# A state-space scan kernel: sums over states by four transposes each, and the token convolution of four chunks on PE

## The chip, the cores and the metric

The kernel runs on one core of one Trainium2 chip. The metric is the device time of one launch in microseconds (us), the median of several runs; a separate execution of the same program is profiled. The engines are PE (TensorE, matmuls; PEld is its loading of weights), DVE (VectorE), ACT (ScalarE), POOL (GpSimd) and SP (SyncE, which issues most DMAs).

## The reference

Four images of 384 channels and 48 x 48 positions pass through four layers, each after a group normalisation and with a residual: a selective state-space block, a block with a patch-wise spectral filter and a 3 x 3 depthwise convolution, an 11 x 11 depthwise convolution, and a mixture of four experts. The change touches the first layer alone (L is 2304 positions, 768 inner channels, 16 states):

```python
xz = xs @ in_proj_w.T
xin, z = jnp.split(xz, 2, axis=-1)
xc = ... # causal convolution over tokens, 4 taps, one filter a channel
xin = jax.nn.silu((xc + conv_b[None, :, None]).transpose(0, 2, 1))
x_dbl = xin @ x_proj_w.T
dt, Bm, Cm = jnp.split(x_dbl, [DT_RANK, DT_RANK + D_STATE], axis=-1)
dt = jax.nn.softplus(dt @ dt_proj_w.T + dt_proj_b)
A = -jnp.exp(A_log)
def step(h_prev, inp):
    x_t, dt_t, B_t, C_t = inp
    dA = jnp.exp(dt_t[..., None] * A)
    dBx = dt_t[..., None] * B_t[:, None, :] * x_t[..., None]
    h_new = dA * h_prev + dBx
    y_t = jnp.einsum('bds,bs->bd', h_new, C_t)
    return (h_new, y_t)
...
y = ys.transpose(1, 0, 2) + xin * D
y = y * jax.nn.silu(z)
out = y @ out_proj_w.T        # then a layer norm over channels
```

All arithmetic is in float32.

## The kernel before

The 2304 positions of an image are cut into five chunks (four of 460, one of 464), and the 768 inner channels into six tiles of 128, taken in three pairs. A list G holds the 20 (image, chunk) items. For each item the generator `scans` runs 96 state steps (`unit`): 3 pairs x 16 states x 2 tiles of the pair. One step is: ACT makes da = exp(dt A) into one of two PSUM banks (L626); POOL multiplies u by the broadcast row B (L630); DVE runs the recurrence (L634) into da or into g; the product with C goes into one of six g buffers, on DVE (L640) for two steps of three and on POOL (L651) for the third; ACT saves the last column for the next chunk (L642, L650). PE then adds g to y: `summed` multiplies it by the identity matrix and accumulates in the PSUM bank of that tile, tag y0 or y1, one buffer each (L600). The skip term xin D is one more matmul of that sum, with a diagonal matrix `d_diag` as weights. Sums of steps that POOL multiplied are held back in `late`. When a pair is done, `gate` (L659) multiplies y in place by the silu of z, on DVE, out of the same bank; the bank is free for the next pair then.

Around the steps, `plan` hangs pieces of other work on step numbers: the tail of the chunk before (`gate` of its last pair, `out_proj`, `layer_norm`, `residual`), `project` and `project_z` for the next chunk and this one, `gates` (the silus, L535 and L538), `expand` and `steps`. In `project`, three matmuls (L490) make the rows of a tile with three tokens of halo in a bank, ACT takes the last tap with the bias (L502), and DVE adds the other three taps (L507, three instructions). `bank` hands out two PSUM banks for all of this. Two more banks serve the other three layers of the image before (`later`, L782) and the experts of the one before that (`experts`, L1090): their pieces are spread over the 480 steps of an image by hand-set weights. So the first image has steps alone, the second has layers two and three beside them, and the third and fourth the experts too. After the last step only layers of the last two images remain.

The code order gives the priority; the framework's scheduler may take a piece that is ready earlier or later than it stands, and each engine then works through its own list in order. `after` fixes the order of two instructions on one engine.

Of the kernel before, what the change touches and what calls it, by code (L numbers as in the profile page):

```python
# [16 lines left out]
P = 128  # L17
# [8 lines left out]
TT = 4  # L26
# [18 lines left out]
def tile_layers(ctx: ExitStack, tc: tile.TileContext, a: dict, out: bass.AP):  # L45
# [218 lines left out]
    with ExitStack() as first:  # L264
# [29 lines left out]
        d_diag = wp.tile([P, MT, P], F32, name="d_diag")  # L294
        for m in range(MT):
            nc.scalar.activation(d_diag[:, m, :], ident, AF.Copy, scale=d_col[:, m : m + 1])
# [117 lines left out]
        def scans(wk, mm):  # L414
# [5 lines left out]
            G = [(b, t) for b in range(NB) for t in range(NC)]  # L420
            st = [{} for _ in G]
# [58 lines left out]
            def project(i, j):  # L480
# [20 lines left out]
                acc = c["xc"][:, j, :n]  # L501
                nc.scalar.activation(  # L502
# [87 lines left out]
            def summed(i, m, lhsT, src):  # L590

                (b, t), c = G[i], st[i]
                n = CHUNKS[t]
                if ("y", m) not in c:
                    c["y", m] = mm.tile(
                        [P, 512], F32, name=f"y{b}_{t}_{m}", tag=f"y{m % 2}", bufs=1
                    )
                    c["terms", m] = 0
                c["terms", m] += 1
                return nc.tensor.matmul(  # L600
                    c["y", m][:, :n],
                    lhsT=lhsT,
                    rhs=src,
                    start=c["terms", m] == 1,
                    stop=c["terms", m] == DS + 1,
                    skip_group_check=True,
                )

            def skip(i, p):

                (b, t), c = G[i], st[i]
                for m in (2 * p, 2 * p + 1):
                    summed(i, m, d_diag[:, m, :], c["xc"][:, m, : CHUNKS[t]])

            def unit(i, m, s):
# [23 lines left out]
                if here is da:  # L639
# [3 lines left out]
                    ins = summed(i, m, ident, g[:, :n])  # L643

                    c["since"] = c.get("since", 0) + 1
                    if late and (c["since"] >= 2 or (m % 2 and s == DS - 1)):
                        after(late.pop(0)(), ins)
                else:
# [3 lines left out]
                    late.append(lambda: summed(i, m, ident, g[:, :n]))  # L652
                    c["since"] = 0

            def gate(i, m):
                (b, t), c = G[i], st[i]
                n = CHUNKS[t]
                zm = c["zs"][:, m, :n]
                nc.vector.tensor_tensor(zm, c["y", m][:, :n], zm, ALU.mult)  # L659
# [56 lines left out]
            def tail(i):  # L716

                for k in range(TT):
                    yield lambda k=k: out_proj(i, k)
                yield lambda: layer_norm(i)  # L720
                for ct in range(CT):
                    yield lambda ct=ct: residual(i, ct)
# [3 lines left out]
            load(0)  # L726
            for j in range(MT):
                project(0, j)
            gates(0, None)
            expand(0)  # L730
            steps(0, 0)
            for i, (b, t) in enumerate(G):
                todo = {}
# [11 lines left out]
                if i:  # L745
                    for m in (MT - 2, MT - 1):
                        plan(0, lambda m=m: gate(i - 1, m))
                    for k, piece in enumerate(tail(i - 1)):
                        plan(3 + 2 * k, piece)
# [13 lines left out]
                for p in range(MT // 2):  # L763
                    if p:
                        for h in range(2):
                            plan(2 * DS * p, lambda m=2 * p - 2 + h: gate(i, m))
                    if p < MT // 2 - 1:
                        plan(2 * DS * p + DS, lambda p=p: steps(i, p + 1))
                    plan(2 * DS * p + DS, lambda p=p: skip(i, p))
                for p in range(MT // 2):  # L770
                    for q in range(2 * DS):
# [3 lines left out]
                        yield b, t, 2 * DS * p + q  # L775
                assert not todo
            for m in (MT - 2, MT - 1):
                gate(len(G) - 1, m)
# [575 lines left out]
```

## Time and profile before

Columns of the shares: busy time of an engine as a share of the span.

| what | value |
|---|---|
| runs | 5764.69, 5762.97, 5753.89 us; median 5762.97 |
| profiled execution | 5767.51 us, span 5765.7 us, 69035 instructions |
| PE, PEld | 5255.3 us (91%), 3320.9 us (58%), 23236 instructions each |
| DVE | 4030.3 us (70%) |
| ACT | 2956.1 us (51%) |
| POOL | 3110.3 us (54%) |
| granted clock of PE, mean | 0.953 |
| sums over states, L600 | 3840 instructions of PE for g, 240 for the skip term |
| state steps, L626 | 1920 exponentials |
| first scan, last exponential start | at 96 us, at 4860 us |

The page adds up busy time over stages of different character; from about 1030 us on, other layers run beside the scan, and from 4870 us on there is no scan. A line such as L600 collects all instructions of one code line, with the shape of their operands, how often they ran, their busy time and mean duration, and the idle time of their engine just before them.

### The profile page before, as it was taken

How to read it: one execution, taken by the hardware profiler on the slowest of the kernel's cores; microseconds unless marked ns; L12 is line 12 of the kernel's file. 1: busy time of each engine (PE TensorE's matmuls, PEld its weight loads, DVE VectorE, ACT ScalarE, POOL GpSimd, SP SyncE). 2: the span in 40 equal slices, each digit the busy share in tenths (PEclk: the TensorE clock that was granted, in tenths of full speed). 3: DMA queues.
4: the chain of work that ended last, by engine and by line, in shares of the span. 5: the costliest groups of instructions: out<-in, count | busy, mean ns of one | idle time of the engine just before them, and what ended most of it. 6: DMA issues, size and time to landing. Idle time of an engine off the chain costs nothing. (4 is left out here: it accounts for less than half of the span.)

```text
span 5765.7 us, 69035 instructions
## 1 busy us (share of the span) xinstructions
PE 5255.3 (91%) x23236; PEld 3320.9 (58%) x23236; DVE 4030.3 (70%) x5653; ACT 2956.1 (51%) x6424; POOL 3110.3 (54%) x2795
## 2 busy tenths in 40 slices
PE   6888888988889999999887999999988799999999
PEld 3333333433455546777433664877634375789999
DVE  5988988899997796666899577656698856451110
ACT  3555555555566654444655565444455564335321
POOL 3877888766586685555565366545465646000000
PEclk9999989988999999999998899999989899899999
DMA  4444444434344363233333235323332323311100
GB/s 135 134 137 135 143 127 139 124 118 121 118 139 137 114 206 108 89 106 112 112 119 106 90 120 171 99 88 102 103 112 95 121 93 125 114 45 43 54 23 26
DMA packets 396011, 634.19 MB, mean 110 GB/s; under 512 B 32373, under 2 KB 386789, under 8 KB 392190
## 3 DMA queue, kind: packets, MB, share of 16 engines
q1 hardware_dynamic: 382148, 618.58, 33.7%
q10 hardware_dynamic: 13498, 11.11, 0.7%
q8 instruction: 184, 3.01, 0.2%
q14 instruction: 181, 1.48, 0.1%
HBM read 571.80 MB, written 57.80 MB: 109 GB/s over the span
## 5 line engine op out<-in xcount | busy, mean ns | idle before, releaser
L630 POOL TENSOR_TENSOR bu<-u,bc 128x460 f32<-128x460 f32 (+1 forms) x1920 | 2217.2, 1167 | 1346.3 <-DVE g L634 632.8
L600 PE MATMUL y<-g,ident 128*128 128x460 f32 (+1 forms) x3840 | 1838.3, 597 | 286.8 <-DVE g L640 282.2
L626 ACT ACTIVATE da<-dt,a_neg 128x460 f32<-128x460 f32 (+1 forms) x1920 | 1232.1, 646 | 268.5 <-DVE g L640 166.2
L634 DVE TENSOR_TENSOR_SCAN da<-da,carry,bu 128x460 f32<-128x460 f32 (+1 forms) x1008 | 1165.7, 1170 | 196.6 <-ACT da L626 170.1
L600 PEld LDWEIGHTS y<-g,ident 128*128 128x128 f32 x3840 | 704.3, 201 | 1008.1 <-DVE g L640 541.7
L651 POOL TENSOR_TENSOR g<-g,bc 128x460 f32<-128x460 f32 (+1 forms) x660 | 766.7, 1162 | 249.4 <-DVE g L634 128.0
L640 DVE TENSOR_TENSOR g<-da,bc 128x460 f32<-128x460 f32 (+1 forms) x1260 | 775.9, 627 | 109.7 <-PE y L600 80.1
L634 DVE TENSOR_TENSOR_SCAN g<-da,carry,bu 128x460 f32<-128x460 f32 (+1 forms) x528 | 617.2, 1169 | 134.1 <-PE y L600 67.9
L1139 PEld LDWEIGHTS ph<-xe,w 128*128 128x128 f32 x4608 | 596.7, 191 | 54.3 <-issue 40.4
L1157 PEld LDWEIGHTS pout<-hr,w 128*128 128x128 f32 x4608 | 591.4, 190 | 54.7 <-issue 43.8
L1139 PE MATMUL ph<-xe,w 128*128 128x144 f32 x4608 | 620.1, 288 | 0.0
L1157 PE MATMUL pout<-hr,w 128*128 128x144 f32 x4608 | 616.4, 287 | 1.5 <-DVE xe L1168 1.5
L642 ACT COPY carry<-da 128x1 f32<-128x1 f32 x1008 | 158.0, 157 | 884.2 <-DVE g L640 882.5
L998 PEld LDWEIGHTS pc<-band,row 128*128 128x128 f32 x3456 | 455.8, 194 | 81.1 <-issue 48.6
L1147 ACT ACTIVATE hr<-ph,nb 128x144 f32<-128x144 f32 x768 | 235.5, 377 | 507.3 <-PE ph L1139 506.9
L998 PE MATMUL pc<-band,row 128*128 128x162 f32 (+14 forms) x3456 | 469.2, 286 | 6.5 <-ACT row L987 4.7
L669 PE MATMUL po<-w_out,zs 128*115 128x384 f32 (+1 forms) x960 | 346.6, 494 | 11.1 <-DVE zs L659 7.7
L878 DVE SCALAR_TENSOR_TENSOR dw<-pad,w_dw,dw 128x384 f32<-128x384 f32 x576 | 342.2, 609 | 14.4 <-ACT pad L866 11.2
L634 DVE TENSOR_TENSOR_SCAN da<-da,nil,bu 128x460 f32<-128x460 f32 x252 | 291.5, 1170 | 74.3 <-ACT da L626 66.4
L490 PE MATMUL pin<-xch,w_inx 128*128 128x463 f32 (+2 forms) x720 | 323.1, 579 | 10.8 <-DVE dt L585 4.7
L518 PE MATMUL pinz<-xch,w_inz 128*128 128x460 f32 (+1 forms) x720 | 306.0, 559 | 12.0 <-DVE xc L507 7.9
L507 DVE SCALAR_TENSOR_TENSOR xc<-pin,conv_w,xc 128x460 f32<-128x460 f32 (+1 forms) x360 | 246.9, 686 | 76.6 <-ACT xc L502 73.9
(170 smaller groups left out, 4754.8 us busy)
## 6 DMA issues: line engine op xcount, KB each, us to landing
bc<-bcd SPq DMA_DIRECT2D x768, 460.0 KB, 3.6
bc<-bcd SPq DMA_DIRECT2D x192, 464.0 KB, 3.6
xs<-x1d SPq DMA_DIRECT2D x24, 576.0 KB, 4.3
x2d<-xs SPq DMA_DIRECT2D x24, 576.0 KB, 2.9
x<-x2d SPq DMA_DIRECT2D x12, 1152.0 KB, 6.5
x3d<-x SPq DMA_DIRECT2D x12, 1152.0 KB, 5.9
xg<-x3d SPq DMA_DIRECT2D x24, 576.0 KB, 4.6
xe<-x3d SPq DMA_DIRECT2D x64, 216.0 KB, 2.6
```

The costliest lines, as they stand in the source:

```text
L490: nc.tensor.matmul(ps[:, lo : halo + n], lhsT=w_inx[:, k, bass.ts(j, P)], rhs=c["x"][:, k, lo : halo + n], start=k == 0, stop=k == CT - 1,)
L600: return nc.tensor.matmul(c["y", m][:, :n], lhsT=lhsT, rhs=src, start=c["terms", m] == 1, stop=c["terms", m] == DS + 1, skip_group_check=True,
L626: nc.scalar.activation(da[:, :n], c["dt", p][:, m % 2, :n], AF.Exp, scale=a_neg[:, m, s : s + 1])
L630: nc.gpsimd.tensor_mul(bu[:, :n], c["u", p][:, m % 2, :n], bc[:, 0, :n])
L634: nc.vector.tensor_tensor_scan(here[:, :n], da[:, :n], bu[:, :n], last if t else nil[:, 0:1], ALU.mult, ALU.add,)
L640: nc.vector.tensor_mul(g[:, :n], here[:, :n], bc[:, 1, :n])
L651: nc.gpsimd.tensor_mul(g[:, :n], here[:, :n], bc[:, 1, :n])
L669: nc.tensor.matmul(ps[:w, :C], lhsT=c["zs"][:, m, bass.ts(k, w)], rhs=w_out0[:, m, :], start=m == 0, stop=m == MT - 1,)
L878: nc.vector.scalar_tensor_tensor(v, src, w_dw[:, ct, k : k + 1], v, ALU.mult, ALU.add)
L998: nc.tensor.matmul(d["acc2"][:, : BANDS[k] * W].rearrange("p (h w) -> p h w", w=W)[:, lo - edges[k] : hi - edges[k], xlo:xhi], lhsT=d["row ...
L1139: nc.tensor.matmul(ps[:, bass.ts(m, EB)], lhsT=d["w1"][:, e, k, bass.ts(m, P)], rhs=d["x", s][:, k, :], start=k == 0, stop=k == CT - 1,)
L1157: nc.tensor.matmul(d["o"][:, bass.ts(m, EB)], lhsT=d["w2"][:, e, k, bass.ts(m, P)], rhs=d["h", s, e][:, k, :], start=e == 0 and m == 0 and ...
```

## The change

The diagonal `d_diag` goes. A new helper `turned` sends a tile to PE as four transposes: each takes a quarter of the columns (115 or 116) as weights, the identity as the moving operand, and adds into the y bank, which now holds tokens on partitions and four blocks of 128 channels. `skip` scales xin by D on ACT into a g buffer and starts the sum with it; it now stands ahead of the pair's steps. The sum of every state step uses `turned`. After the pair's last step `collect` moves the two y banks to SBUF on ACT, and `gate`, a few steps later, transposes them back into one of the two shared banks and multiplies there. In chunks 1 to 4 of the first image, `project` has ACT copy the rows with their halo to SBUF, PE apply the four taps with diagonal matrices (24 of them, made once by ACT), and ACT add the bias.

```diff
-        d_diag = wp.tile([P, MT, P], F32, name="d_diag")
-        for m in range(MT):
-            nc.scalar.activation(d_diag[:, m, :], ident, AF.Copy, scale=d_col[:, m : m + 1])
...
                 acc = c["xc"][:, j, :n]
+                if "diag" in taps and t:
+                    row = taps["pool"].tile([P, halo + TM], F32, name=f"row{b}_{t}_{j}", tag="row")
+                    nc.scalar.copy(row[:, : halo + n], ps[:, : halo + n])
+                    qs = bank(f"pcv{b}_{t}_{j}")
+                    for k in range(DCONV):
+                        nc.tensor.matmul(
+                            qs[:, :n],
+                            lhsT=taps["diag"][:, j, k, :],
+                            rhs=row[:, k : k + n],
+                            start=k == 0,
+                            stop=k == halo,
+                        )
+                    nc.scalar.activation(
+                        acc, qs[:, :n], AF.Identity, bias=d["cb"][:, j : j + 1]
+                    )
+                    return
...
-            def summed(i, m, lhsT, src):
+            def turned(y, src, n, start, stop):
+
+                w = n // TT
+                return [
+                    nc.tensor.matmul(
+                        y[:w, bass.ts(k, P)],
+                        lhsT=src[:, bass.ts(k, w)],
+                        rhs=ident,
+                        is_transpose=True,
+                        start=start and k == 0,
+                        stop=stop,
+                        skip_group_check=True,
+                    )
+                    for k in range(TT)
+                ]
+
+            def skip(i, p):
...
+                for h in range(2):
+                    m = 2 * p + h
+                    y = c["y", m] = mm.tile(
+                        [P, 512], F32, name=f"y{b}_{t}_{m}", tag=f"y{h}", bufs=1
+                    )
+                    dx = wk.tile([P, TM], F32, name=f"dx{b}_{t}_{m}", tag="g", bufs=6)
+                    nc.scalar.activation(
+                        dx[:, :n], c["xc"][:, m, :n], AF.Copy, scale=d_col[:, m : m + 1]
+                    )
+                    turned(y, dx, n, True, False)
...
-                    ins = summed(i, m, ident, g[:, :n])
-
-                    c["since"] = c.get("since", 0) + 1
-                    if late and (c["since"] >= 2 or (m % 2 and s == DS - 1)):
-                        after(late.pop(0)(), ins)
+                    ins = turned(c["y", m], g, n, False, s == DS - 1)
+
+                    c["since"] += 1
+                    if late and (c["since"] == 2 or (m % 2 and s == DS - 1)):
+                        for one in late.pop()():
+                            after(one, ins[-1])
                 else:
...
-                    late.append(lambda: summed(i, m, ident, g[:, :n]))
+                    late.append(lambda: turned(c["y", m], g, n, False, s == DS - 1))
                     c["since"] = 0
+
+            def collect(i, p):
+                (b, t), c = G[i], st[i]
+                w = CHUNKS[t] // TT
+                for h in range(2):
+                    m = 2 * p + h
+                    yt = c["yt", m] = wk.tile([P, 512], F32, name=f"yt{b}_{t}_{m}", tag="yt")
+                    nc.scalar.copy(yt[:w, :], c["y", m][:w, :])
 
             def gate(i, m):
...
+                ps = bank(f"pyb{b}_{t}_{m}")
+                for k in range(TT):
+                    nc.tensor.transpose(
+                        ps[:, bass.ts(k, w)], c["yt", m][:w, bass.ts(k, P)], ident[:w, :w]
+                    )
                 zm = c["zs"][:, m, :n]
-                nc.vector.tensor_tensor(zm, c["y", m][:, :n], zm, ALU.mult)
+                nc.vector.tensor_tensor(zm, ps[:, :n], zm, ALU.mult)
...
+            taps["diag"] = taps["pool"].tile([P, MT, DCONV, P], F32, name="diag", bufs=1)
+            for j in range(MT):
+                for k in range(DCONV):
+                    nc.scalar.activation(
+                        taps["diag"][:, j, k, :], ident, AF.Copy, scale=conv_w[:, j, k : k + 1]
+                    )
             for i, (b, t) in enumerate(G):
+                if b == 1 and t == 0:
+                    taps.clear()
+                    first_image.close()
...
                 if i:
-                    for m in (MT - 2, MT - 1):
-                        plan(0, lambda m=m: gate(i - 1, m))
                     for k, piece in enumerate(tail(i - 1)):
-                        plan(3 + 2 * k, piece)
+                        plan(2 + 2 * k, piece)
...
-                            plan(2 * DS * p, lambda m=2 * p - 2 + h: gate(i, m))
+                            plan(2 * DS * p + 3 + 3 * h, lambda m=2 * p - 2 + h: gate(i, m))
                     if p < MT // 2 - 1:
                         plan(2 * DS * p + DS, lambda p=p: steps(i, p + 1))
-                    plan(2 * DS * p + DS, lambda p=p: skip(i, p))
                 for p in range(MT // 2):
+                    skip(i, p)
                     for q in range(2 * DS):
                         unit(i, 2 * p + q % 2, q // 2)
                         for piece in todo.pop(2 * DS * p + q, []):
                             piece()
                         yield b, t, 2 * DS * p + q
+                    collect(i, p)
```

`tail` now begins with the two gates of the last pair, two steps apart.

More of the change, by code (lines that the diff above doesn't have):

```diff
@@ L420, in scans @@
             G = [(b, t) for b in range(NB) for t in range(NC)]
+            first_image = ExitStack()
             st = [{} for _ in G]
@@ L588, in steps @@
                     nc.gpsimd.tensor_mul(u[:, h, :n], dt[:, h, :n], c["xc"][:, 2 * p + h, :n])
-            def summed(i, m, lhsT, src):
+            def turned(y, src, n, start, stop):
[13 more added lines that the diff above has]
+            def skip(i, p):
                 (b, t), c = G[i], st[i]
                 n = CHUNKS[t]
-                if ("y", m) not in c:
-                    c["y", m] = mm.tile(
-                        [P, 512], F32, name=f"y{b}_{t}_{m}", tag=f"y{m % 2}", bufs=1
-                    )
[L598 to L613, printed above, removed]
+                for h in range(2):
+                    m = 2 * p + h
+                    y = c["y", m] = mm.tile(
+                        [P, 512], F32, name=f"y{b}_{t}_{m}", tag=f"y{h}", bufs=1
+                    )
+                    dx = wk.tile([P, TM], F32, name=f"dx{b}_{t}_{m}", tag="g", bufs=6)
[3 more added lines that the diff above has]
+                    turned(y, dx, n, True, False)
             def unit(i, m, s):
@@ L657, in gate @@
                 n = CHUNKS[t]
+                w = n // TT
+                ps = bank(f"pyb{b}_{t}_{m}")
[3 more added lines that the diff above has]
+                    )
                 zm = c["zs"][:, m, :n]
-                nc.vector.tensor_tensor(zm, c["y", m][:, :n], zm, ALU.mult)
+                nc.vector.tensor_tensor(zm, ps[:, :n], zm, ALU.mult)
             def out_proj(i, k):
@@ L716, in tail @@
             def tail(i):
+                yield lambda: gate(i, MT - 2)
+                yield lambda: gate(i, MT - 1)
                 for k in range(TT):
@@ L726, in scans @@
             load(0)
+            taps = {"pool": first_image.enter_context(tc.tile_pool(name="taps", bufs=2))}
             for j in range(MT):
@@ L775, in scans @@
                         yield b, t, 2 * DS * p + q
+                    collect(i, p)
                 assert not todo
-            for m in (MT - 2, MT - 1):
-                gate(len(G) - 1, m)
             for piece in tail(len(G) - 1):
```

## The prediction

> **What bounds the kernel now.** I read the busy table by stretches first, because the page's averages (PE 91%, DVE 70%) mix stages. I cut the span where the character of the work changes.
>
> ```profile
> core 0: us, PE busy (x) PEld busy (x) DVE busy (x) ACT busy (x) POOL busy (x), PEclk, DMA share, GB/s
> 110.00:1030.00 920.00, 758.77 (x1793) 325.71 (x1794) 817.85 (x1019) 497.76 (x1051) 760.24 (x677) 0.94 0.43 135
> 1030.00:1700.00 670.00, 591.59 (x1736) 283.92 (x1735) 615.74 (x877) 394.89 (x845) 455.22 (x410) 0.93 0.40 123
> 1700.00:2200.00 500.00, 478.57 (x1877) 271.65 (x1876) 418.17 (x551) 312.93 (x643) 366.86 (x327) 0.98 0.46 149
> 2200.00:2750.00 550.00, 547.69 (x3069) 417.13 (x3068) 341.11 (x447) 252.73 (x630) 293.25 (x263) 0.99 0.33 101
> 2750.00:3250.00 500.00, 418.66 (x1198) 202.10 (x1197) 425.94 (x623) 278.08 (x572) 289.58 (x261) 0.88 0.36 112
> 3250.00:3600.00 350.00, 341.65 (x1567) 213.28 (x1567) 246.61 (x336) 210.65 (x410) 199.91 (x177) 0.99 0.41 134
> 3600.00:4150.00 550.00, 547.78 (x3072) 418.87 (x3071) 335.50 (x438) 252.71 (x630) 294.14 (x263) 0.99 0.31 97
> 4150.00:4600.00 450.00, 372.23 (x936) 165.75 (x935) 399.66 (x579) 245.44 (x498) 269.68 (x243) 0.89 0.34 110
> 4600.00:4850.00 250.00, 241.93 (x1362) 177.36 (x1361) 170.48 (x211) 170.16 (x339) 149.90 (x132) 0.99 0.33 108
> ```
>
> Columns: stretch, length, busy time and count of each engine, granted clock, DMA. There are three kinds. In 2200 to 2750 and 3600 to 4150 (experts beside the scan) PE is busy all but 2 us of 550: PE time is kernel time. In 1700 to 2200, 3250 to 3600 and 4600 to 4850 PE is busy 96 to 98%, which counts latencies too; DVE's chain shares the limit. Elsewhere DVE leads: 818 of 920 us (89%) in the first image, POOL close behind with 760 (83%), PE 759 (82%).
>
> How many state steps (one exponential of L626 each) fall into the PE-led stretches, from that line's busy time alone:
>
> ```profile
> 1700.00:2200.00 500.00, 145.25 (x227) 0.98 0.46 149
> 2200.00:2750.00 550.00, 117.48 (x182) 0.99 0.33 101
> 3250.00:3600.00 350.00, 77.99 (x122) 0.99 0.41 134
> 3600.00:4150.00 550.00, 117.48 (x182) 0.99 0.31 97
> 4600.00:4870.00 270.00, 64.44 (x101) 0.99 0.34 112
> ```
>
> 364 steps where PE is full, 450 where it is nearly so, 1106 in DVE-led stretches.
>
> **What one sum costs PE.** The groups come next, for the counts:
>
> ```profile
> L600 PE MATMUL y<-g,ident 128*128 128x460 f32 (+1 forms) x3840 | 1838.3, 597 | 286.8 <-DVE g L640 282.2
> L626 ACT ACTIVATE da<-dt,a_neg 128x460 f32<-128x460 f32 (+1 forms) x1920 | 1232.1, 646 | 268.5 <-DVE g L640 166.2
> ```
>
> 1920 steps, but 3840 matmuls: one float32 matmul of the code runs as two instructions. A transpose runs as one: the code of L979 issues 4 images x 3 tiles x 12 rows x 6 = 864, and 864 are listed. A mean duration holds latency that the next instruction overlaps, so I take the pitch from merged timeline rows (start, length): length less one duration, divided by count less one.
>
> ```profile
> 2051.29 1.72 PE L600 MATMUL y<-g,ident 128*128 128x464 f32 x4
> 5422.11 0.82 PE L979 MATMUL pr<-ident,rep 128*128 128x128 f32 x6
> 311.41 0.56 PE L704 MATMUL pt<-ident,on 115*128 115x115 f32 x4
> ```
>
> Today: (1.72 - 0.55)/3 = 0.39 us an instruction, 0.386 at 460 columns, so 0.772 a sum. A transpose with 128 moving columns, the form of the new sum: (0.82 - 0.27)/5 = 0.109. With 115 moving columns, the form of the way back: 0.098. The pitch follows the moving columns though both load 128 weight columns, so narrower weights don't help. Four transposes: 0.436, **0.336 less** a sum. A chunk saves 96 + 6 (skip) times 0.336 = 34.3 and pays 24 x 0.098 = 2.4 for the way back: 31.9 us of PE, 0.332 a step.
>
> The Trainium skill, "TensorE: Matmul & The Clock Gate", section Terms, calls the transpose mode four times faster for FP32. By that a sum's 512 columns would take an estimated 0.21 us and the full stretches would save some 200 us instead of 121; the row of L979 shows a factor of two (0.109 us for 128 columns against twice 128 x 0.386/460 = 0.107), and I go by the row.
>
> **The parts, added up.**
>
> 1. Full PE stretches: 364 x 0.332 = 121 us. DVE at 341 of 489 us does not take over there. Bounds 90 and 121; I take 90%, **-109**, for waits that show once PE has gaps.
> 2. Nearly full stretches: 75, 41 and 34 us of PE time. DVE at its best share seen (89%) would need 470, 277 and 192 us, so at most 30, 41 and 34 = 105 come through. I take 80%, **-83**; bounds 40 and 105.
> 3. DVE-led stretches behind the first image: PE loses 207 us that lay beside DVE. Only DVE's waits for PE (L910 and L848, about 50 us in all there) can gain: **-20**, bounds 0 and -50.
> 4. Convolution in chunks 1 to 4 of the first image.
>
> ```profile
> L507 DVE SCALAR_TENSOR_TENSOR xc<-pin,conv_w,xc 128x460 f32<-128x460 f32 x288 | 197.2, 685 | 65.5 <-ACT xc L502 63.0
> L659 DVE TENSOR_TENSOR zs<-y,zs 128x460 f32<-128x460 f32 x96 | 58.8, 627 | 35.1 <-ACT zs L538 23.6 <-PE y L600 10.6
> ```
>
> DVE loses 18 x 0.685 = 12.3 us a chunk, 49 in four. PE gains 24 x 2 x 0.386 = 18.5 us a chunk, covered by the 31.9 it saves; without them its 32 us of idle time would just hold it. ACT swaps an evacuation of 0.73 us (L502) for a row copy (0.55, as L581) and a plain one (0.64, as L525): 11 us at 54% busy. Bounds 0, if POOL or ACT takes over, and 49/0.89 = 55; I take two thirds, **-36**, because POOL's 760 us still fit into 884. On PE the four matmuls wait for the row copy with sums queued behind; DVE feels that only once six g buffers are full.
> 5. ACT's new work: six scaled copies a chunk (607 ns for 384 columns at L1106, so 0.67 for 460) and six moves of y (476 ns for 384 at L987, so 0.60 for 512): 7.6 us, 152 in all, in front of the exponentials that DVE needs:
>
> ```profile
> DVE da L634 <- ACT da L626: 236.5, 236, 11.4
> ```
>
> (total us, times, longest). At a pair's end ACT, in order, also waits until PE has summed the last state, and the next pair's skip transposes wait for the moves, as its first sum waits for the gates today. If none of the next exponentials went ahead, DVE would be late by a sum, two moves, two copies and an exponential: 0.7 + 1.2 + 1.3 + 0.65 = 3.9 us; if two did, nothing. Today's gates show both ends: 0.05 us at 406.51, 4.7 behind the long silu. I take 1 us at the 1106/32 = 34 pair ends of DVE-led stretches: **+34**, bounds 0 and 133. The gates move 3 and 6 steps later and can give back up to the 35 us idle of L659; **-15**, because DVE starves for exponentials during the silu anyway.
> 6. Once: 24 diagonals at 0.30 us pitch (two at L296 in 0.69) into the 5.5 us that ACT waits for PE at L558: **+2**. Gates hold one of two shared banks 120 times for about a microsecond: **+3**, bounds 0 and 60. No DMA is added.
>
> Sum: -109 - 83 - 20 - 36 + 34 - 15 + 5 = **-224 us** on the profiled execution of 5767.5 us (span 5765.7, 1.8 around it), 4.5 over the median of the runs. On the median 5763.0: **5540 us**.
>
> **The rivals.**
>
> Smaller gain: PE's relief runs into the chain of ACT and DVE. Parts 1 and 2 at 90 and 40, part 3 and 4 at 0 and 20, pair ends at 50: -90 - 40 - 20 + 50 = -100, **5660 us**. For it: 236 waits of DVE for ACT, most of them in PE-led stretches. Against: ACT is at 46% where PE is full.
>
> Larger gain: every part at its good end: -121 - 105 - 50 - 55 - 35 = -366, **5400 us**. For it: sums leave g and y earlier. Against: DVE's 89% is a share kept over 900 us.
>
> Slower: the clock. After a stretch with gaps on PE the granted clock halves:
>
> ```profile
> 3220.60:3224.00 3.40, 2.31 (x21) 1.94 (x19) 0.89 (x2) 3.40 (x8) 0.17 (x1) 1.00 0.00 0
> 3224.00:3227.40 3.40, 3.40 (x14) 2.54 (x13) 1.70 (x4) 2.48 (x7) 2.13 (x2) 0.51 0.01 2
> ```
>
> The first image needs some 129 us of PE at full clock a chunk (matmul pitches added up), afterwards 129 - 31.9 + 18.5 = 115. If the clock stayed at half, that is 230 us against chunks of 184: +46 x 5; the other DVE-led stretches would go PE-bound too, by about 130 + 20 + 20. With -192 of parts 1 and 2: +208, **5970 us**; it decides once over half of those stretches is at half clock (now 0.88 to 0.94). Against: a backlog on PE keeps PE busy, and the rows above show the full clock wherever it is. The same page, section Part 4: PE-mode transpose, holds that transposes don't count as busy for the clock, which would speak for it; no row has enough transposes in a run to test it.
>
> That accumulating transposes are no cheaper than the pitch of L979 says can't be seen beforehand; 10% on the pitch takes back 0.044 x 814 = 36 us.
>
> **How the numbers follow.** Forecast 0.54, smaller 0.21, larger 0.17, slower 0.06, nothing measurable 0.02 (under 0.2%, 11 us, can't be told from none here). Faster 0.92, same 0.02, slower 0.06. The range reaches half way into both neighbours and leaves the slower case out: 5420 to 5680.
>
> **What would show it.** Right: groups of four transposes at a pitch near 0.109, single instructions; the stretches of full PE shorter by 50 to 60 us each; the first image shorter by 20 to 55 us with DVE's share kept. Wrong: a pitch of 0.2 (two instructions a transpose), a granted clock under 0.8 over the first image with PE then at its limit, or DVE's waits for ACT grown by more than 100 us.

## The result, and the profile after

The changed kernel takes 5825.05 us (median of 4 runs, 5818.99 to 5829.08) against 5762.28 us for the kernel before on the same chip: a ratio of 1.0111, 95% interval 1.0093 to 1.0128. It is 1.1% slower. The forecast was 5540 us, faster; the time lies outside the range of 5420 to 5680.

The head of the page after: the span, the busy time of each engine, the granted clock in 40 slices, and the group of the new sums.

```profile
span 5826.1 us, 78782 instructions
PE 4977.6 (85%) x27988; PEld 3845.1 (66%) x27988; DVE 3995.9 (69%) x5581; ACT 3079.2 (53%) x6706; POOL 3110.5 (53%) x2795
PEclk9788878688789988999878799899979699899999
L608 PE MATMUL y<-ident,g 128*115 128x128 f32 (+1 forms) x7680 | 1278.8, 314 | 405.9 <-DVE g L660 404.5
```

PE did get the work off: 278 us less busy, the sums' group 1279 us in place of 1838. The span grew by 60 us all the same, and the idle time of PE in front of the sums grew from 287 to 406 us. The table by stretches, at the cuts shown of before (length, busy time and count of PE, PEld, DVE, ACT, POOL, granted clock, DMA share, GB/s):

```profile
110.00:1030.00 920.00, 697.03 (x2879) 473.16 (x2877) 720.32 (x871) 504.10 (x1075) 692.81 (x620) 0.81 0.40 125
1030.00:1700.00 670.00, 525.08 (x2087) 337.16 (x2088) 592.79 (x846) 374.46 (x760) 433.95 (x390) 0.80 0.38 119
1700.00:2200.00 500.00, 424.27 (x2549) 329.18 (x2548) 424.80 (x539) 338.12 (x724) 380.06 (x338) 0.93 0.42 134
2200.00:2750.00 550.00, 525.21 (x3497) 446.33 (x3496) 373.92 (x495) 285.68 (x694) 330.60 (x292) 0.95 0.39 124
2750.00:3250.00 500.00, 381.11 (x1598) 245.62 (x1597) 414.43 (x605) 266.22 (x549) 272.35 (x249) 0.82 0.33 106
```

In the first stretch DVE does 720 us of work in 920, where it did 818: POOL and PE are idle with it, and the clock is 0.81 in place of 0.94. PE is no longer full from 2200 on, yet DVE gained little there. Fixed times cut through different work in the two kernels, so I also cut by work. The k-th exponential of the state steps starts state step k (0 to 1919, 96 to a chunk, 480 to an image), and the table gives the time from one step number to another in the profiled executions; the experiments' columns are explained below.

| state steps | leads before | before | after | e1 | e7 | e9 | e13 | e16 |
|---|---|---|---|---|---|---|---|---|
| 0 to 480, first image | DVE | 932 | 1002 | 977 | 939 | 940 | 933 | 933 |
| 480 to 672, windows | DVE | 453 | 481 | 475 | 459 | 476 | 453 | 453 |
| 672 to 1056 | PE, nearly | 903 | 910 | 910 | 868 | 884 | 887 | 872 |
| 1056 to 1152 | PE | 299 | 271 | 271 | 272 | 267 | 267 | 267 |
| 1152 to 1344, windows | DVE | 558 | 594 | 587 | 547 | 599 | 561 | 557 |
| 1344 to 1440 | PE, nearly | 266 | 241 | 240 | 262 | 236 | 267 | 258 |
| 1440 to 1632 | PE | 569 | 534 | 535 | 510 | 516 | 512 | 513 |
| 1632 to 1824, windows | DVE | 546 | 573 | 573 | 543 | 574 | 547 | 548 |
| 1824 to 1919 | PE, nearly | 241 | 226 | 215 | 238 | 210 | 234 | 233 |

After against before: the five rows led by PE give 96 us back; the four led by DVE take 161. Where it went is told by what each engine waits for. PE, all of the changed kernel (total us, times, longest):

```profile
PE y L608 <- DVE g L660: 404.5, 323, 6.4
PE y L608 <- ACT yt L682: 84.4, 33, 9.1
```

The second line has no counterpart before: PE stands 84 us for the moves of y (yt, L682), once for 9.1. And DVE in the first image, from 93 to 1090 us:

```profile
DVE da L654 <- ACT da L646: 41.6, 27, 7.6
DVE g L654 <- PE y L608: 41.4, 5, 12.1
DVE g L654 <- POOL bu L650: 20.9, 33, 1.9
DVE g L660 <- PE y L608: 20.5, 11, 3.9
```

Before, it waited 10 us there for exponentials and none of the longest twelve waits was for PE's sums. "g waits for PE y" means that all six g buffers were full, five times for 8 us on the mean. The row of DVE's waits for exponentials grew from 236.5 to 329.1 us over the whole kernel, close to the 100 us that the prediction named as a sign of being wrong. One place where PE stands for a move, in ACT's and PE's rows of the timeline (start, length, in brackets the idle time ahead and who ended it):

```profile
3703.67 1.28 ACT L549 ACT_TABLE_LOAD   x1
3704.97 2.50 ACT L549 ACTIVATE xc<-xc 128x2760 f32<-128x2760 f32 x1
3707.38 2.48 ACT L552 ACTIVATE zs<-zs 128x2760 f32<-128x2760 f32 x1
3709.88 1.28 ACT L408 ACT_TABLE_LOAD   x1
3711.17 1.07 ACT L682 COPY yt<-y 115x512 f32<-115x512 f32 x2
```

```profile
3703.19 0.90 PE L1183 MATMUL ph<-xe,w 128*128 128x144 f32 x6
3711.81 1.41 PE L608 MATMUL y<-ident,dx 128*115 128x128 f32 x5 [7.72 <-ACT yt L682]
```

Here is one mechanism. Once a chunk the two long silus and their table loads hold ACT for 7.5 us, right at the end of the first pair. The moves come behind them in ACT's list. The skip sums of the next pair (y<-ident,dx) are next in PE's list and need the bank that the moves free. So PE stands 7.7 us; in the first image the g buffers fill meanwhile and DVE stops too. The same place in the first image, PE's row and DVE's:

```profile
581.06 2.05 PE L608 MATMUL y<-ident,dx 128*115 128x128 f32 x8 [7.64 <-ACT yt L682]
582.33 1.17 DVE L654 TENSOR_TENSOR_SCAN g<-da,carry,bu 128x460 f32<-128x460 f32 x1 [8.56 <-PE y L608]
```

Before, DVE read y in place, and the skip sums stood in mid-pair. PE's stand alone does not stop DVE, though. In e1 below, where the convolution is back on DVE, PE stands even longer at this place, but what DVE waits for is an exponential, which stands behind the same silus and moves in ACT's list. PE's row and DVE's, then DVE's waits in e1 from 93 to 1090 us:

```profile
567.39 2.05 PE L608 MATMUL y<-ident,dx 128*115 128x128 f32 x8 [9.37 <-ACT yt L682]
568.63 2.25 DVE L654 TENSOR_TENSOR_SCAN da<-da,carry,bu 128x460 f32<-128x460 f32 x2 [6.21 <-ACT da L646]
```

```profile
DVE da L654 <- ACT da L646: 42.1, 19, 7.6
DVE g L660 <- PE y L608: 2.2, 4, 0.7
```

So the 62 us of full g buffers go with the convolution (56 us in e2, which has no moves); the late exponentials go with the pair ends.

### The profile page after: what moved, and what is told of

It reads as the page before. It is cut to its first block, busy times and chain, and to the rows that moved or that the text cites. A ratio compares the mean times of both kernels' runs of the same rounds, so it can differ in the third digit from the quotient of the medians.

```text
span 5826.1 us, 78782 instructions
## 1 busy us (share of the span) xinstructions
PE 4977.6 (85%) x27988; PEld 3845.1 (66%) x27988; DVE 3995.9 (69%) x5581; ACT 3079.2 (53%) x6706; POOL 3110.5 (53%) x2795
## 5 line engine op out<-in xcount | busy, mean ns | idle before, releaser
L608 PE MATMUL y<-ident,g 128*115 128x128 f32 (+1 forms) x7680 | 1278.8, 314 | 405.9 <-DVE g L660 404.5
L608 PEld LDWEIGHTS y<-ident,g 128*115 128x115 f32 (+1 forms) x7680 | 1097.3, 199 | 697.6 <-DVE g L660 557.1
L1042 PE MATMUL pc<-band,row 128*128 128x162 f32 (+14 forms) x3456 | 492.8, 293 | 10.3 <-DVE x L1060 8.4
L532 PE MATMUL pinz<-xch,w_inz 128*128 128x460 f32 (+1 forms) x720 | 321.5, 580 | 28.7 <-DVE dt L599 9.4
L671 ACT COPY carry<-g 128x1 f32<-128x1 f32 x528 | 100.9, 191 | 402.9 <-DVE g L654 401.4
```

The lines of the kernel that those rows point to most:

```text
L608: nc.tensor.matmul(y[:w, bass.ts(k, P)], lhsT=src[:, bass.ts(k, w)], rhs=ident, is_transpose=True, start=start and k == 0, stop=stop, skip ...
L1042: nc.tensor.matmul(d["acc2"][:, : BANDS[k] * W].rearrange("p (h w) -> p h w", w=W)[:, lo - edges[k] : hi - edges[k], xlo:xhi], lhsT=d["row ...
```

## The experiments

Three theories at the start. CLOCK: with less to do PE falls to half clock, and the slow transposes make DVE wait. PAIR END: what the change puts between two pairs costs more than the sums save. CONVOLUTION: PE has no room for it where it was put. Each run lists the kernel that it edits, and ratios are to the kernel before on the same chip. That kernel took 5762 to 5772 us on the chips used, so the difference of two runs' times is good to some 10 us; the ratios are safer.

**e1: the change without its convolution.**

```diff
-            taps = {"pool": first_image.enter_context(tc.tile_pool(name="taps", bufs=2))}
+            taps = {}
```

> The changed kernel with the convolution of all chunks back on DVE; all else as changed. Theory CLOCK (transposes keep PE less busy, its granted clock falls to half in the DVE-led stretches, and late sums and projections hold DVE up): the clock of the first image stays near 0.8, its length does not fall by more than 20 us, total 5810 to 5880. Theory CONV (the four diagonal matmuls, with two shared banks each, hold up the projections of the first image): the first image is 50 us or more shorter than in the changed kernel, total 5750 to 5780. Theory PAIR END (moves of y, scaled copies and gates in the order of ACT and the shared banks): first image longer by up to 49 us, total 5830 to 5880.

Measured 5786.82 us, ratio 1.0028 (1.0016 to 1.004), granted clock 0.877; first image 977 us. So 38 us of the loss are the convolution's (48 by the ratios), and the turned sums without it still gain nothing. The total lies in none of the three ranges.

**e2: the convolution alone, on the kernel before** (the change's lines of `project`, with the sums, skip and gates of before).

```diff
+                if "diag" in taps and t:
+                    row = taps["pool"].tile([P, halo + TM], F32, name=f"row{b}_{t}_{j}", tag="row")
...
+                    nc.scalar.activation(
+                        acc, qs[:, :n], AF.Identity, bias=d["cb"][:, j : j + 1]
+                    )
+                    return
```

> The kernel before with the convolution of chunks 1 to 4 of the first image on PE as in the change, sums by identity matmuls as before. CONV: the first image is 50 us or more longer than before, total 5810 to 5840. CLOCK and PAIR END: PE has 18.5 us more a chunk at a clock of 0.94, DVE 12.3 us less, so the first image is 10 to 50 us shorter, total 5715 to 5755.

Measured 5808.19 us, ratio 1.0064 (1.004 to 1.0088), granted clock 0.957; first image 968 us (+36), all later rows unchanged. Why it costs instead of saving 36 shows in two parts of one chunk, projections and rest. First the kernel before, then e2 (columns as above):

```profile
276.00:386.00 110.00, 97.07 (x237) 42.25 (x236) 93.36 (x124) 63.66 (x133) 79.11 (x72) 0.95 0.42 135
386.00:457.00 71.00, 52.03 (x114) 21.89 (x114) 67.74 (x80) 36.78 (x93) 67.61 (x61) 0.93 0.44 139
```

```profile
276.00:386.00 110.00, 102.14 (x268) 46.27 (x266) 79.18 (x104) 62.75 (x128) 71.70 (x64) 1.00 0.38 119
386.00:457.00 71.00, 53.39 (x113) 21.19 (x113) 66.66 (x77) 36.84 (x93) 69.05 (x63) 0.93 0.45 143
```

PE's idle time of a chunk, 32 us, is there, but 19 of it in the second part. The projections stand in the first, where PE is busy 97 of 110 us, and the convolution joins them: DVE is busy 14 us less there, 12 of them the convolution that it no longer does, and 44 state steps start in this part instead of 49. Cut by work, steps 12 to 36 of the first four chunks take 74 us on the mean, 64 before; steps 36 to 60 hardly differ (39.4 and 39.6).

**e3: the four transposes as plain matmuls** (of the changed kernel).

```diff
-                        is_transpose=True,
```

> The changed kernel with the four transposes of each sum run as ordinary float32 matmuls with the identity: same operands, same layout, same moves and gates, two instructions each, so 0.87 us of PE a sum instead of 0.44. CLOCK: the granted clock of the first image goes back to 0.9 or more and the first image is at least 30 us shorter although PE has more work; the PE-led stretches cost 814 x 0.44 = 350 us at most, total 5950 to 6200. PAIR END: the first image is as long as in the changed kernel or longer, the clock being back or not; total 6050 to 6250.

Measured 6088.72 us, ratio 1.0557 (1.0536 to 1.0579), clock 0.954. The clock is back and the kernel is 264 us slower than the change: PE's time counts, the clock by itself doesn't help.

**e4: the changed kernel, plus a zero matmul a step in the first image.**

```diff
+                    nc.tensor.matmul(
+                        y[:w, : n // 2], lhsT=cold[:, :w], rhs=src[:, : n // 2],
+                        start=False, stop=False, skip_group_check=True,
+                    )
```

> The changed kernel with one more matmul ahead of each sum in the first image: zero weights, half of the columns of g moving, added into y, so nothing changes in the result and PE does 0.39 us more a step (480 steps). CLOCK: the clock of the first image goes back to 0.9 or more, and the first image is 30 to 65 us shorter, total 5760 to 5800. CONV and PAIR END: no shorter, since PE has only more to do; total 5820 to 5860.

Measured 5852.78 us, ratio 1.0145 (1.0128 to 1.0162); the share of low clock in the first image fell from 39% to 11%, and the first image grew from 1002 to 1034 us. Against CLOCK, but PE's full first part of the chunk could have hidden a gain; hence e5.

**e5: the same zero matmul on e1, in all chunks that DVE leads.**

```diff
+        LED = [(0, t) for t in range(NC)] + [(1, 0), (1, 1), (2, 2), (2, 3), (3, 2), (3, 3)]
-                    ins = turned(c["y", m], g, n, False, s == DS - 1)
+                    ins = turned(c["y", m], g, n, False, s == DS - 1, (b, t) in LED)
```

> The changed kernel without its convolution on PE, plus one matmul with a zero weight over half of each g (added to y, so the sums stay) in every state step of the chunks where VectorE leads: all of the first image, chunks 0 and 1 of the second, 2 and 3 of the third and fourth. Compared with e1_conv_on_dve. CLOCK (PE now does too little in these chunks, its clock drops, and the slow transposes make VectorE wait): the granted clock rises from 0.877 to 0.92 or more and the stretches get shorter in spite of the added work, the first image 977 -> about 940, steps 1152 to 1344 587 -> about 562, steps 1632 to 1824 573 -> about 550; the whole about 5710 against 5787. PAIR END (what the change puts between two pairs, the skip copies, the moves, the way back, is what VectorE waits for): the clock rises, the stretches stay within 10 us or get longer; the whole 5780 to 5840.

Measured 5807.95 us, ratio 1.0068 (1.0047 to 1.0089), clock 0.93; first image 983 (e1: 977), steps 1152 to 1344 590 (587), 1632 to 1824 563 (573). The clock is back and nothing is won in these rows but 10 us in the last, as PAIR END had it.

**e6: the moves alone, on the kernel before** (sums by the identity matmul).

```diff
+                    nc.scalar.copy(yt[:, :n], c["y", m][:, :n])
-                nc.vector.tensor_tensor(zm, c["y", m][:, :n], zm, ALU.mult)
+                nc.vector.tensor_tensor(zm, c["yt", m][:, :n], zm, ALU.mult)
```

> The kernel before, sums by the identity matmul, with only the moves of the change: ACT copies both y banks to SBUF at the end of a pair, and the gates run from there at the change's later places. The clock stays as before (0.95 or more). PAIR END: the first image gets 30 to 45 us longer (932 -> 962 to 977), the stretches 1152 to 1344 and 1632 to 1824 20 to 30 us longer, the whole about 5850 to 5880. CLOCK: every one of these stretches within 10 us of before, the whole 5760 to 5790. If the later gates free VectorE from a wait, as the prediction had it, up to 15 us less: 5755.

Measured 5824.09 us, ratio 1.0091 (1.0068 to 1.0113), clock 0.946; first image 954 (+22). With no transposed sum in it this kernel is about as slow as the change. It is not the moves alone, though: the gate, which here reads y from SBUF, takes 879 ns on the mean (median 639, longest 1639) where it took 628 before, 30 us of DVE over 120 gates. The size is less than PAIR END expected (1152 to 1344 +11, 1632 to 1824 -9), and the gates that come later gave nothing back.

**e7: e1 without moves and way back.** The gates read the turned sums in place.

```diff
-                zm = c["zs"][:, m, :n]
-                nc.vector.tensor_tensor(zm, ps[:, :n], zm, ALU.mult)
+                zm = c["zs"][:w, m, :n]
+                nc.vector.tensor_tensor(zm, c["y", m][:w, :n], zm, ALU.mult)
```

> The changed kernel without its convolution on PE, and without moves and way back: the gates read the turned sums directly, at the places where they stood before. Left out: the turning back, so that the gating is of a wrong layout and of 115 or 116 partitions alone. The four transposes a state and the skip copies stay. CLOCK: the low clock stays, the first image as in e1 (965 to 985 us), the whole 5770 to 5795. PAIR END: the first image 935 to 945, the stretches 1152 to 1344 and 1632 to 1824 as before (558 and 546), the shorter PE-led stretches kept, the whole 5660 to 5700.

Measured 5624.93 us, ratio 0.9745 (0.9725 to 0.9765), clock 0.886. This settles CLOCK against PAIR END: at the low clock of e1 the rows led by DVE are those of before (939, 459, 547, 543 against 932, 453, 558, 546). Moves, way back and later gates cost 5787 - 5625 = 162 us, more than PAIR END expected (the whole is 35 us under its range).

**e8: e2 with ten g buffers.**

```diff
-                g = wk.tile([P, TM], F32, name=f"g{v_}", tag="g", bufs=6)
+                g = wk.tile([P, TM], F32, name=f"g{v_}", tag="g", bufs=10)
```

> The kernel before with the convolution on PE (e2_conv_alone: first image 968, whole 5808), but ten g buffers in place of six. CONV BY FULL BUFFERS (the sums stand behind the convolution's and projection's groups in PE's list, g stays full, VectorE waits): VectorE's waits for PE in the first image fall from 60 to under 30 us, the first image 968 -> about 940, the whole about 5780. Rival (the convolution delays xc, the row copies delay ACT's exponentials, or VectorE's 60 us of waits only move to another place): first image 960 to 970, the whole 5795 to 5815.

Measured 5792.78 us, ratio 1.0033 (1.0023 to 1.0044); first image 972 us, DVE's waits for PE's sums with g still 62 us in it (56 in e2). My expectation failed: the wait is no matter of depth. The 15 us came in later rows, which the convolution doesn't touch.

**e9: e1 with another order on ACT and PE.** Each bank is moved right ahead of the first sum that needs it, behind the next pair's first two exponentials; skip copies and sums stand in mid-pair, in buffers of their own; gates two steps later.

```diff
+                if m % 2 in owed:
+                    owed.pop(m % 2)()
+                y = c["y", m] = mm.tile(
-                    skip(i, p)
+                    plan(2 * DS * p + 10, lambda p=p: skip(i, p))
+                    plan(2 * DS * p + DS, lambda p=p: skip_sum(i, p))
-                    collect(i, p)
+                        owed[h] = lambda i=i, m=2 * p + h: collect(i, m)
```

> The changed kernel without its convolution on PE, whole and with every sum, with ACT's order at a pair's end changed: the move of each y bank stands behind the first two exponentials of the next pair (right ahead of the first sum that needs the bank), the skip copies stand in mid-pair, in two buffers of their own, and the gates come two steps later. ACT ORDER (in the changed kernel ACT stands at the pair's end until PE has the last sum, then does two moves and two skip copies before the first exponential, and VectorE runs dry): VectorE's waits for exponentials fall from 42 us in the first image to below 20, the first image is 940 to 955 us, the whole 5640 to 5700. WAY BACK (it is the 24 transposes back a chunk and the gates behind them that VectorE and PE pay for, which are all still here): the first image stays at 965 to 980, the whole at 5760 to 5800.

Measured 5689.36 us, ratio 0.9867 (0.9851 to 0.9884): 98 us better than e1 (93 by the ratios) by order and two more buffers, and faster than the kernel before. The waits of PE's sums for the moves fall from 81 to 21 us, DVE's for exponentials in the first image from 42 to 13. What is left of WAY BACK is at most the 64 us to e7. The clock once more, from the start of the scan to 932 us, in the kernel before and then in e9:

```profile
110.00:932.00 822.00, 686.62 (x1638) 297.51 (x1639) 723.17 (x909) 452.16 (x981) 664.40 (x592) 0.94 0.42 134
```

```profile
110.00:932.00 822.00, 620.93 (x2589) 433.11 (x2590) 726.25 (x908) 469.81 (x1025) 666.09 (x594) 0.78 0.41 132
```

DVE does the same work in the same time at a clock of 0.78 as at 0.94.

**e10: e1 with the skip copies and sums in mid-pair, moves at the pair's end.**

```diff
-                    skip(i, p)
+                    plan(2 * DS * p + 10, lambda p=p: skip(i, p))
+                    plan(2 * DS * p + DS, lambda p=p: skip_sum(i, p))
```

> As e1_conv_on_dve (5787), but only the skip copies are put in mid-pair, with two buffers of their own; the moves stay at the pair's end, ahead of the next pair's exponentials. ACT ORDER: two of the four instructions that stand between the last sum and the next exponential are gone (2 x about 0.4 us at 57 pairs, 46 us, where VectorE leads): the whole 5740 to 5765. WAY BACK: no change, 5775 to 5795.

Measured 5733.52 us, ratio 0.9952 (0.9937 to 0.9967): more than expected (there are 60 pair ends, not the 57 of the expectation, but that is not it). The waits of PE's sums for the moves go from 81 to 43 us, but the transposes back now wait 26 us for them, 7 in e1.

**e11: e9 with the skip copies at the pair's start** (their sums in mid-pair).

```diff
-                    plan(2 * DS * p + 10, lambda p=p: skip(i, p))
+                    skip(i, p)
```

> As e9_moves_late, but the skip copies stay at the pair's start, ahead of its first exponentials (in buffers of their own). ACT ORDER: the wait for the last sum is away from ACT's queue, two copies stay that wait for nothing; the whole 10 to 30 us above e9, 5655 to 5720. WAY BACK: as e1, 5760 to 5800.

Measured 5693.86 us, ratio 0.9876 (0.9856 to 0.9896), like e9. ACT's two copies cost nothing measurable where they stand; the 10 to 30 us expected for them did not show.

**e14: e1 with buffers of their own for the skip copies, nothing moved.**

```diff
-                    dx = wk.tile([P, TM], F32, name=f"dx{b}_{t}_{m}", tag="g", bufs=6)
+                    dx = wk.tile([P, TM], F32, name=f"dx{b}_{t}_{m}", tag="dx")
```

> As e1_conv_on_dve (5787), with one thing changed: the skip copies take two buffers of their own instead of two of the six of g; copies and their sums stay at the pair's start. BUFFERS (the copies at the pair's start take g buffers that VectorE needs): as e10_skip_mid, 5725 to 5750. SUMS AT THE START (the transposed copies stand in PE's list ahead of everything else of the pair and wait there for the bank that the move frees): no change, 5775 to 5795.

Measured 5768.96 us, ratio 0.999 (0.9977 to 1.0003): 18 of e10's 53 us are the two g buffers (22 of 44 by the ratios). The rest, 22 to 35 us, is most likely the skip sums' place in PE's list: e11 clears the copies, though in e9's order and not in e10's.

**e15: e1 with the silus behind the first pair's moves.**

```diff
+                            if "moved" in c:
+                                after(one, c["moved"])
-                plan(28, lambda: gates(more, i))
+                plan(33, lambda: gates(more, i))
```

> As e1_conv_on_dve (5787; PE waits 81 us for the moves in all), with one order changed: once a chunk the two long silus with their table loads (1.3 + 2.5 + 2.5 + 1.3 us) stand behind the moves of the first pair in ACT's list, not ahead of them; the first pair's gates come two steps later for it. SILU (the moves of the first pair wait behind the silus, PE's list stands behind the moves, because the skip sums of the next pair are next in it): PE's waits for the moves fall from 81 to below 35 us, the first image 977 -> 945 to 955, the whole 5730 to 5755. Rival (ACT's stand at every pair's end, not the silus): PE's waits for the moves stay over 60 us, the whole 5775 to 5795.

Measured 5765.47 us, ratio 0.9993 (0.998 to 1.0005); first image 964. PE's waits, whole kernel:

```profile
PE y L610 <- DVE g L662: 420.1, 352, 5.5
PE y L610 <- ACT yt L684: 31.4, 33, 3.2
```

The long waits are gone (longest 3.2 us, 9.4 in e1), so the silus were what made the moves late. It is less than SILU expected for the time: 50 us of PE's waiting were worth 21 of time, for the gates wait for the silus again (23 us of DVE in the first image, as before the change).

**e12: e2 with the convolution's matmuls behind the projections**, at steps 34 to 44, rows kept in six buffers, a silu of its own at step 46.

```diff
+                    for j in range(MT):
+                        plan(34 + 2 * j, lambda j=j: convolve(more, j))
+                    plan(46, lambda: gates(more, None))
+                    plan(52, lambda: expand(more))
```

> The kernel before with the convolution on PE in chunks 1 to 4 of the first image (e2_conv_alone: first image 968 us, whole 5808), but the rows are kept (six row buffers) and the four diagonals' matmuls planned at steps 34 to 44 of the chunk, behind the projections, with a SiLU of its own for them at step 46. PLACE (the convolution's 18.5 us of PE a chunk fell into the one third of a chunk in which PE has no idle time): steps 12 to 36 fall from 74 us a chunk in e2 to about 63, steps 36 to 60 grow by 2 to 6, the first image 925 to 945, the whole 5755 to 5785. Rival (the convolution on PE costs what it costs wherever it stands, or the second SiLU and its table change take the gain): first image 960 to 975, the whole 5795 to 5815.

Measured 5781.51 us, ratio 1.0024 (1.0013 to 1.0034); first image 944. 24 of the 36 us were the place. The gain did not come, for a new wait stands there, DVE from 100 to 1020 us:

```profile
DVE da L657 <- ACT da L649: 59.4, 41, 5.5
DVE zs L682 <- ACT zs L561: 10.2, 3, 4.4
DVE g L663 <- PE y L623: 9.7, 8, 3.3
```

The waits of g for PE's sums are down from 56 us in e2 to 16 (two rows, 9.7 and 6.1); ACT's exponentials are late instead (25 us in e2, 10 before). By work, steps 12 to 36 now take 60 us a chunk, but steps 36 to 60 take 48, 40 before. Whether by the second silu or by the copies is not shown.

**e13: transposes, as in e9, only in the nine chunks beside experts and norms; elsewhere all as before.**

```diff
+            TURN = [(1, 2), (1, 3), (1, 4), (2, 0), (2, 1), (2, 4), (3, 0), (3, 1), (3, 4)]
+                if G[i] not in TURN:
+                    return [nc.tensor.matmul(
+                        y[:, :n], lhsT=lhsT, rhs=src[:, :n],
```

> A version that may beat both: the four transposes a state (as in e9_moves_late, with the late moves) only in the nine chunks beside the experts and the norms behind them, where PE leads (chunks 2 to 4 of the second image, 0, 1 and 4 of the third, 0, 1 and 4 of the fourth); in the first image and beside the windows, where VectorE leads, the identity matmul, the diagonal for D and the gates of the kernel before. The convolution is VectorE's as before. By the differences of e9's profile to before in the nine chunks alone (steps 672 to 1056 -19, 1056 to 1152 -32, 1344 to 1440 -30, 1440 to 1632 -53, 1824 to 1919 -31, together -165): the whole 5600 to 5640 if the loss beside the windows (+23, +41, +28 in e9) is made by the moves and the way back there. If that loss comes from the transposed chunks ahead of them instead (work that PE finishes earlier in one place and lacks in the next), it stays, and the whole is 5670 to 5700.

Measured 5655.1 us, ratio 0.9794 (0.978 to 0.9808). The rows beside the windows are back at 453, 561 and 547: their loss in e9 is made in those chunks. The time is 15 us over the range expected, since of the 30 and 31 us of steps 1344 to 1440 and 1824 to 1919 nothing and 7 came. In e9 these two rows had gained 30 and 31 right behind rows that lost 41 and 28, so much of that gain was time shifted from one row to the next.

**e16: e13 with e15's order in its nine chunks.**

```diff
-                plan(28, lambda: gates(more, i))
+                plan(35 if G[i] in TURN else 28, lambda: gates(more, i))
```

> As e13_where_pe_leads (5655), with the silus behind the first pair's moves in its nine transposed chunks. There PE waits for the moves only 5 us in all, so SILU expects little: 5640 to 5660. If ACT's exponentials profit from the shorter stand (VectorE's waits for them in the nine chunks are about 150 us), down to 5625; if the later gates hold up the tail of the chunk, 5665.

Measured 5631.44 us, ratio 0.976 (0.9747 to 0.9773), the best of the runs that leave nothing out: 137 us under the kernel before. The page's busy line:

```profile
PE 5031.8 (89%) x25288; PEld 3448.6 (61%) x25288; DVE 4010.3 (71%) x5653; ACT 2998.0 (53%) x6532; POOL 3108.3 (55%) x2795
```

PE is busier here than in the changed kernel and the span is 197 us shorter: its time was saved only where it leads.

## Why the prediction was wrong

By its own parts:

- **The price of a sum was right.** Successive transposes start 0.109 us apart at full clock (median of some 5200 pairs of the trace), and each is one instruction.
- **Parts 1 and 2 (-109 - 83 = -192)** were right in mechanism, and part 2 was too large. The five rows led by PE gave 96 us in the changed kernel, 128 in e7, which has no moves and no way back. (The 165 of e9 hold what its windows' rows had lost; in e13 the five give 112.) In e7 the two rows where PE was full gave 27 + 59 = 86 of the 96 us that 288 steps of 0.332 us make, 90%, as part 1 took. The other three gave 35 + 4 + 3, about 43, for some 106 forecast (part 2's 83 and the rest of part 1). In steps 672 to 1056, by far the longest of the three, the granted clock fell too, from 0.97 to 0.93 in e7, and DVE's waits for exponentials stayed, 36 us where there were 47; which of them held the gain down is not shown.
- **Part 3 (-20)** was lost in the pair ends: the windows' rows cost +28, +36 and +27 us. In e7 they are at +6, -11 and -3: nothing to gain, nothing lost.
- **Part 4 (-36)** measured +36 alone. The step that failed reads "covered by the 31.9 it saves; without them its 32 us of idle time would just hold it": both are of a whole chunk, and the work was planned into the part of it where PE has 13 us idle in 110. "DVE feels that only once six g buffers are full" was true, and they were full. At a better place (e12) the first image is still 12 us longer than before: then DVE waits 59 us for exponentials, 10 before, which part 4 put at nothing.
- **Part 5 (+34 - 15, bounds 0 and 133)** is the step that turned the sign. It priced how late DVE's next exponential would be at a pair's end, "1 us at 34 pair ends", and gave the silus' 4.7 us to the gates of before only. It left out that the moves stand behind those same silus in ACT's list, and that PE's list then stands behind the moves: "the next pair's skip transposes wait for the moves" was written down and got no price. e1 less e7 is 162 us, over the bound of 133 and against a net 19; 98 of it go with e9's order and two buffers. The silus ahead of the moves are not the whole of it: putting them behind (e15) took PE's waits from 81 to 31 us and gave back 21 of the 162. What DVE pays shows in e1's first image, 45 us longer than before: it waits 32 us more for exponentials, 13 for the transposes back and 12 more for ACT's copies of the last column. The 23 us that the gates had waited for the silus are gone there, but no run shows the 15 us of time back that part 5 had for that.
- **Part 6** can't be told apart.

The miss is 5825 - 5540 = 285 us: the convolution 38 + 36 = 74, pair ends and way back 162 - 19 = 143, and the rest of parts 1 to 3, 212 forecast against 144 in e7, 68; each is good to some 10 us.

Of the rivals, "slower: the clock" got the sign, not the cause. The clock did fall (0.883 over the span, 0.953 before), and e5 and e7 show that in the rows led by DVE it cost nothing that can be measured. In the rows that PE nearly leads it fell as well (steps 672 to 1056: 0.97 before, 0.90 after), and no run shows what that cost. "Smaller gain" named ACT's and DVE's chain and raised the pair ends, but only to 50 us; none of the rivals was a wait of PE for ACT.

Open: why the windows' rows cost 23 to 41 us in e9 and nothing in e7. In the later two of the three rows DVE's waits for exponentials are higher (36 and 39 us against 13 and 23), which points to the moves among ACT's other work; in the first they are alike (7 and 6), and DVE waits 11 us for PE's sums with g instead. No run took the way back away alone.

## What to carry to other kernels

When a result gets a new reader on another engine, price the wait of whoever needs the buffer next by everything that stands ahead of the reader in its engine's list, long instructions first; move the first writer back as well. "PE has 32 us idle a chunk" covers added work only in the part of the chunk where the idle time is. A cheaper form that costs others something belongs only in the stages where the relieved engine leads: e16 against e1 is 155 us for choosing nine chunks of twenty and an order.

## What the hardware showed

Transposes bring PE's full clock back. In the changed kernel, PE from 740 us on, and the granted clock (last but two of the columns) of three stretches:

```profile
740.52 5.18 PE L608 MATMUL y<-ident,g 128*115 128x128 f32 x25
745.54 2.48 PE L532 MATMUL pinz<-xch,w_inz 128*128 128x460 f32 x6
```

```profile
737.40:740.80 3.40, 3.23 (x11) 1.60 (x11) 3.40 (x5) 2.08 (x6) 3.14 (x3) 0.62 0.00 0
740.80:744.20 3.40, 3.40 (x17) 3.40 (x17) 2.78 (x5) 3.27 (x7) 2.04 (x2) 0.50 0.74 211
744.20:747.60 3.40, 3.40 (x16) 2.42 (x15) 3.40 (x5) 0.38 (x1) 3.40 (x4) 0.87 0.35 135
```

From 740.5 PE runs nothing but transposes, at half clock, 0.213 us apart; by the clock's record the full clock returns at 745.1, still inside the run of transposes, and the last of them are 0.109 apart. The trace has more such places, at 342.3 and 543.7 us for instance, where PE ran nothing but transposes of g in the 3.4 us before. The Trainium skill, "TensorE: Matmul & The Clock Gate", section Part 4: PE-mode transpose, says that the full clock doesn't engage for them; the prediction could not test it, and this trace disagrees. The factor of four for FP32 that its section Terms gives is about two here: 0.109 us for 128 columns, where an identity matmul of the kernel before takes 2 x 0.107.

Also unexpected: with half clock for 46% of the first image's time (e9; 13% before) its length is 940 us where it was 932, and DVE's work in it takes the same time.
